# A four-layer graph network: layer 1's first part moved into the edge loop of layer 0

## The chip, the cores and the metric

The kernel runs on one core of a Trainium2 chip. A core has a matrix engine (TensorE, PE in the profile, with its weight loads listed as PEld), a vector engine (VectorE, DVE), an engine for functions (ScalarE, ACT), a general engine (GpSimd, POOL), and SyncE (SP), which here only issues transfers. Each engine works through its own queue in order and waits on semaphores for the others. The metric is device time in microseconds (us), the median of several runs.

## The reference, cut to what matters

There are 4096 nodes with 512 features, and 65536 edges (src, dst). Four layers follow one another, each with a layer norm and a relu ahead of it and its result added to x:

```python
# layer 0
h = relu(layernorm(x)); x = x + gat(h, src, dst)      # 8 heads, then softmax over the 512 features
# layer 1
h = relu(layernorm(x)); x = x + gcn(h)                # relu((D^-1/2 A D^-1/2 h) @ W)
# layer 2
h = relu(layernorm(x)); x = x + message_passing(h)    # two dense layers on every edge
# layer 3
h = relu(layernorm(x)); x = x + gcn_by_destination(h)
```

Layer 0 gives each source node a softmax-weighted sum over its distinct edges: a numerator of 512 columns, a denominator for each of 8 heads. What layer 1 needs for a block of 128 nodes before any edge can be summed, called **layer 1's first part** here, is: numerator by denominator, softmax over the features, add x, layer norm, relu, product with the 512 x 512 weight, and scaling by the root of the node's degree. The result is a row of the table `ytab`, which layer 1's edge loop gathers.

## The kernel before, in words

Nodes are held in 32 blocks (NB) of 128 (P). `acc` is an SBUF array of 32 blocks x 522 columns: 512 sums, 8 denominators, 2 degree columns. Edges are sorted by source in a sorting network that runs beside the first projection. In the 512 columns (tiles) of 128 sorted edges each, 8 tiles make a group of the layer 0 edge loop: 64 groups, in source order, so that group g's sources lie in a window of 128 consecutive nodes, and these windows move forward through the blocks. A window can straddle two blocks, which is why a group is added to `acc` twice (`add_window`, L424), each time with a mask, at a block number read from a register.

`attend` is that loop. Its order is written by hand; within it each engine's queue is the order of the calls. In the step for group g:

- `fetch(g+3)`: 8 indirect gathers on POOL (through the helper `gather`, L412) into `rows`, which has four buffers.
- `turn(g+1)`: PE turns 8 one-hot matrices (L623) into two PSUM banks named `t_ps`; `turned` casts them on ACT (`oh_t`, L631) and selects the source's scores (`of`, L635 on ACT, L636 on DVE).
- `weigh(g, j)`: DVE multiplies two tiles' rows by their weights for 6 heads (L678); `weigh_last` does the other 2 heads on ACT (L672).
- `add_up(j)`: PE adds two tiles to `sum_ps` (L684), for j = 0, 2, 4, 6. These are the four pairs of sums of a group.
- `keep(g-1)`: DVE adds the previous group's sums to `acc` (L424).
- `one_hots(g+2)`: one DVE instruction (L407).
- `source_parts(g+1)`: 8 short matmuls into `e_ps` (L644), after the second pair of sums. `scores(g+1)` reads them on DVE (L650 to L656) and takes the exponent on ACT (L657), and `weights(g+1)` writes the weights (L664, L665), at the end of the step.

So the last product of a group (`weigh(g, 6)`) stands on DVE behind the scores of the next group, and the last pair of sums on PE stands behind that product.

After the loop `layer1_begins` does layer 1's first part in eight rounds of four blocks: it divides (L793), takes the maximum (L795) and the exponent (L798, with the sum of the row as a second output, read by an instruction of its own), adds x (L800), stores x1 (L801), takes mean and variance (L349), norms (L377), turns (L384, L386), multiplies by the weight (`product`, L401), scales (L809) and stores the row of `ytab` (L810). It runs between the two edge loops; no gather runs beside it.

Then `sum_edges` for layer 1 gathers from `ytab` (L412), sums on PE (L768) and adds with `add_window`. Beside it run `Between` (layer 1's end and layer 2's first product, block by block) and `by_destination` (the edge lists in the order of the destination), as generators that are advanced after every second tile.

Of the kernel before, what the change touches and what calls it, by code (L numbers as in the profile page):

```python
# [20 lines left out]
P = 128  # L21
# [13 lines left out]
def kernel(  # L35
# [57 lines left out]
    acc = keep_pool.tile([P, NB, DA], F32, name="acc")  # L93
    dis = keep_pool.tile([P, NB], F32, name="dis")

# [15 lines left out]

    ends = src_pool.tile([P, 2, W], I32, name="ends")
    sg = src_pool.tile([P, 8], F32, name="sg")
    turns = src_pool.tile([P, 7, P], F32, name="turns")
    ones = src_pool.tile([P, P], F32, name="ones")
    shift = src_pool.tile([P, P], F32, name="shift")
    p_f = src_pool.tile([P, 1], F32, name="p_f")

    x1 = dram.tile([N, D], F32, name="x1")
# [136 lines left out]
    def by_destination(pool, ppool):  # L256

        three = pool.tile([P, 3, W], F32, name="three_d")
        for j in range(2):
# [46 lines left out]
    class Side:  # L306


        def __init__(self, *work):
            self.work = list(work)  # L310
# [238 lines left out]
    with tc.tile_pool(name="sort", bufs=1) as sp, tc.tile_pool(name="sort_ps", bufs=1, space=PSUM) as spp, \  # L549
# [28 lines left out]
        nc.vector.tensor_copy(odd[:, 2:3], widest)  # L578
        nc.sync.dma_start(nodes, node.rearrange("p b k h -> p (b k h)"))

    node3 = node_pool.tile([P, NB, 3, 2 * H], BF16, name="node3")
    with tc.tile_pool(name="parts", bufs=1) as lp:
        rest = lp.tile([P, NB, 2 * H], F32, name="rest")
        nc.vector.tensor_copy(rest, node[:, :, 0:2, :].rearrange("p b c h -> p b (c h)"))
        for k in range(3):
            nc.vector.tensor_copy(node3[:, :, k, :], rest)
            if k < 2:
                nc.vector.tensor_sub(rest, rest, node3[:, :, k, :])

    GT = 8  # L590
    ACT_HEADS = 2
# [3 lines left out]
    def attend(ctx):  # L595
        if True:
# [3 lines left out]
            kept = ctx.enter_context(tc.tile_pool(name="edge_keep", bufs=1, space=PSUM))  # L600
            both_ps = kept.tile([P, P + 2 * GT * H], F32, name="both_ps")
            ids_ps = both_ps[:, :P]
            w_ps = both_ps[:, P:].rearrange("p (k t h) -> p k t h", k=2, t=GT)
            nc.scalar.copy(ids_ps, row_i)
# [85 lines left out]


            rows, ohs, sums = {}, {}, {}
            for g in range(-3, groups + 1):
                now = lambda k: 0 <= k < groups
# [35 lines left out]
    one2 = node_pool.tile([P, 2], F32, name="one2")  # L730
# [46 lines left out]

    ytab = dram.tile([N, D], F32, name="ytab")
    def layer1_begins():
# [31 lines left out]

    layer1_begins()
    ptab = dram.tile([N, D], F32, name="ptab")
# [637 lines left out]
```

## Time and profile before

| | us |
|---|---|
| median of 3 runs | 5849.13 (5844.71 to 5850.42) |
| the profiled execution's own time | 5524.6 |
| its span | 5522.8 |
| PE busy in the span | 5110.0 (93%) |
| DVE busy | 3529.2 (64%) |
| ACT busy | 3323.5 (60%) |
| POOL busy | 2910.0 (53%) |
| sums of layer 0's edge loop (L684), first and last start | 256.1 and 897.6 |
| first sum of layer 1's edge loop (L768) | 1067.8 |

Rows of the profile give line, engine, operation, output and inputs, shapes and count; then busy time and the mean duration of one in ns; then the idle time of the engine ahead of these instructions, and what ended it. "issue" is idle time in which the engine waited for nothing that the profile shows. A 32-bit matmul of this kernel appears as two instructions. Matmuls overlap in the queue, so that the mean duration of one is longer than the time that it adds.

### The profile page before, as it was taken

Reading aid. Unit: us, or ns where it says so; the run is one execution under the profiler, and the core shown is the slowest. Engines: PE = TensorE matmul, PEld = TensorE weight load, DVE = VectorE, ACT = ScalarE, POOL = GpSimd, SP = SyncE. Lnnn points to the kernel's source line nnn. Section 1 sums busy time; section 2 is a strip of 40 time slices with the busy share of each in tenths; the row PEclk is TensorE's granted clock in tenths of the full one; section 3 lists DMA queues with packets and bytes.
Section 4 is the critical chain, followed back from the end, with each engine's and each line's share of the span. In section 5 each row is a group of like instructions: output and inputs, shape, how many; then the busy total and the mean of one; then the engine's idle time right before and its main releaser. Section 6 shows DMA issues by size and latency. Waiting matters only on the chain.

```text
span 5522.8 us, 56347 instructions
## 1 busy us (share of the span) xinstructions
PE 5110.0 (93%) x17274; PEld 2739.2 (50%) x17274; DVE 3529.2 (64%) x5696; ACT 3323.5 (60%) x5015; POOL 2910.0 (53%) x2604
## 2 busy tenths in 40 slices
PE   6788887899998999999999999999999899988887
PEld 4477775344443455555555555555555566622222
DVE  8688888333333677777777777777777465633333
ACT  1255555344443788888888888888888434333343
POOL 0177772277774655555555555555554111157776
PEclk9899999999999999999999999999999999999999
DMA  3377775588885655555555555555554211167787
GB/s 103 100 214 214 214 214 180 184 263 269 261 263 180 145 114 114 114 114 114 114 115 114 115 114 115 115 114 114 114 114 84 77 69 65 58 192 210 236 252 222
DMA packets 344871, 841.72 MB, mean 152 GB/s; under 512 B 60272, under 2 KB 76656, under 8 KB 344560
## 3 DMA queue, kind: packets, MB, share of 16 engines
q0 software_dynamic: 237568, 673.35, 49.6%
q1 hardware_dynamic: 106992, 164.66, 8.7%
q8 instruction: 141, 2.31, 0.2%
q14 instruction: 170, 1.39, 0.1%
HBM read 752.62 MB, written 85.20 MB: 152 GB/s over the span
## 4 chain that ended last, share of the span: by engine, by line
PE 69%; DMA 6%; POOL 4%; issue 2%; DVE 1%; ACT 1%; DVEq 0%; SPq 0%; POOLq 0%; ACTq 0%
PE m_ps L401 32%; PE sum_ps L768 9%; DMA g<-ztab,d_src 5%; PE small_ps L967 4%; PE small_ps L994 4%; PE o_ps L401 4%; PE tr_ps L974 4%; PE u_ps L1159 4%; PE pq_ps L868 4%; POOL g L412 4%; PE tr_ps L957 1%; PE tr L1134 1%; PE y_ps L401 1%; DMA g<-ytab,s_dst 0%; ACT h_t L1136 0%
## 5 line engine op out<-in xcount | busy, mean ns | idle before, releaser
L401 PE MATMUL m_ps<-w_sb,h_t 128*128 128x512 f32 x4096 | 1820.8, 592 | 0.5 <-ACT h_t L976 0.5
L401 PEld LDWEIGHTS m_ps<-w_sb,h_t 128*128 128x128 f32 x4096 | 757.5, 190 | 809.1 <-issue 797.8
L768 PE MATMUL sum_ps<-g,oh 128*128 128x512 f32 x2048 | 1026.3, 617 | 135.5 <-DMA g<-ztab,d_src 90.2
L412 POOL DMA_INDIRECT pg<-ptab,d_src x512 | 496.6, 970 | 986.6 <-ACT h_t L976 809.7
L950 POOL DMA_INDIRECT pg<-qtab,d_dst x512 | 880.7, 1720 | 156.4 <-issue 144.1
L768 PEld LDWEIGHTS sum_ps<-g,oh 128*128 128x128 f32 x2048 | 355.7, 191 | 745.0 <-issue 342.4
L412 POOL DMA_INDIRECT rows<-htab,s_dst x512 | 484.5, 946 | 394.3 <-issue 376.7
L412 POOL DMA_INDIRECT g<-ytab,s_dst x512 | 486.0, 949 | 355.6 <-DMA x_mid<-x 180.5
L412 POOL DMA_INDIRECT g<-ztab,d_src x512 | 485.2, 948 | 239.4 <-issue 118.2
L684 PE MATMUL sum_ps<-rows,oh 128*128 128x261 f32 x2048 | 502.8, 393 | 98.7 <-DVE rows L678 98.7
L976 ACT COPY h_t<-tr_ps 128x512 f32<-128x512 f32 x512 | 275.2, 589 | 429.3 <-PE tr_ps L974 429.2
L424 DVE SCALAR_TENSOR_TENSOR acc<-sum_ps,d_half,acc 128x512 f32 x256 | 192.3, 751 | 444.8 <-PE sum_ps L768 425.6
L684 PEld LDWEIGHTS sum_ps<-rows,oh 128*128 128x128 f32 x2048 | 378.0, 192 | 179.0 <-DVE rows L678 124.9
L1026 DVE TENSOR_TENSOR pg<-pg,small_ps 128x512 f32<-128x512 f32 x512 | 318.6, 683 | 186.7 <-PE small_ps L967 150.1
L424 DVE SCALAR_TENSOR_TENSOR acc<-sum_ps,s_half,acc 128x522 f32 (+1 forms) x256 | 193.2, 755 | 375.5 <-PE sum_ps L768 334.4
L994 PE MATMUL small_ps<-parts,oh 128*128 128x512 f32 x1024 | 310.7, 446 | 13.4 <-DVE oh L407 13.4
L988 DVE TENSOR_TENSOR parts<-z,parts 128x1024 fp32r<-128x1024 f32 x256 | 313.6, 1225 | 8.8
L974 PEld LDWEIGHTS tr_ps<-ident,pg 128*128 128x128 f32 x2048 | 240.6, 142 | 145.6 <-issue 145.6
L424 DVE SCALAR_TENSOR_TENSOR acc<-small_ps,d_half,acc 128x512 f32 x256 | 192.3, 751 | 171.6 <-PE small_ps L994 152.3
L1063 DVE TENSOR_TENSOR pg<-pg,qg 128x1024 f32<-128x1024 f32 x256 | 301.4, 1219 | 0.7 <-ACT qg L1060 0.7
L1150 POOL TENSOR_TENSOR h_sb<-h_sb,b_bc 128x1024 f32<-128x1024 f32 x16 | 37.7, 2355 | 453.8 <-PE tr L1134 428.8
L974 PE MATMUL tr_ps<-ident,pg 128*128 128x128 f32 x2048 | 266.3, 273 | 10.8 <-DVE pg L1063 10.8
(278 smaller groups left out, 7982.2 us busy)
## 6 DMA issues: line engine op xcount, KB each, us to landing
xt<-in_x_dram SPq DMA_DIRECT2D x16, 1024.0 KB, 5.8
eg<-in_edge_attr_dram SPq DMA_DIRECT2D x128, 128.0 KB, 2.7
htab<-acc SPq DMA_DIRECT2D x32, 256.0 KB, 2.0
rows<-htab,s_dst POOLq DMA_INDIRECT x512, 3.8
x<-xt SPq DMA_DIRECT2D x8, 1024.0 KB, 4.3
ytab<-acc SPq DMA_DIRECT2D x32, 256.0 KB, 2.1
x_mid<-x SPq DMA_DIRECT2D x32, 256.0 KB, 5.5
g<-ytab,s_dst POOLq DMA_INDIRECT x512, 4.6
```

The lines of the kernel that those rows point to most:

```text
L401: nc.tensor.matmul(ps, h_t[:, k, :], w_sb[:, k0 + k, :], start=start and k == 0, stop=stop and k == KC - 1)
L412: nc.gpsimd.indirect_dma_start(out=dst_ap, out_offset=None, in_=table, in_offset=bass.IndirectOffsetOnAxis(ap=idx, axis=0))
L424: nc.vector.scalar_tensor_tensor(at, ps, half[:, k, i:i + 1], at, op0=OP.mult, op1=OP.add)
L684: nc.tensor.matmul(ps[:, c, :HW], oh[:, j + k, :], rows[:, j + k, c * HW:(c + 1) * HW], start=j + k == 0, stop=j + k == GT - 1)
L768: nc.tensor.matmul(ps, oh[:, j, :], g[:, j, :], start=i % per == 0 and j == 0, stop=i % per == per - 1 and j == U - 1)
L950: nc.gpsimd.indirect_dma_start(out=pg[:, j, :], out_offset=None, in_=qtab, in_offset=bass.IndirectOffsetOnAxis(ap=d_dst[:, t:t + 1], axis= ...
L974: nc.tensor.transpose(h_ps[:, k, :], h[:, j, k * P:(k + 1) * P], ident)
L976: nc.scalar.copy(h_t, h_ps)
L988: nc.vector.tensor_sub(parts[:, 1], m, parts[:, 0].bitcast(F32))
L994: nc.tensor.matmul(ps, oh[:, j, :], parts[j // 2][:, k, j % 2, :], start=j == 0 and k == 0, stop=j == U - 1 and k == 1)
L1026: nc.vector.tensor_add(nxt[:, j], nxt[:, j], ps)
L1063: nc.vector.tensor_mul(h[i][:, half], h[i][:, half], qg[:, half])
```

## The change

Layer 1's first part is no longer called after the edge loop. It is cut into 13 steps per block (class `Block`), and a plan places each step in the loop of `attend`: how many groups after the block's begin, and at which of six places in the step. Block b begins in the step for group 2b + 3, at the latest in that for group 64; six steps without edge work follow the last group so that the last blocks are finished. A block's transposes ("turn") and its product ("multiply") stand at the place "between", which is after the third pair of sums and ahead of the last. PSUM banks for both come from the two `t_ps` buffers. The arithmetic differs in places: the norm's mean comes from a sum that the addition of x gives as a second output, and the variance from a square on ACT with a summed output; norm and relu are one ACT instruction; the roots of variance and degree are taken together, two columns wide, in `scales`, whose second column is now `dis`. x is loaded and x1 stored block by block.

The sort's temporary tiles move to a pool of their own that is closed after the projection, so `by_destination` loads `ends` again.

```diff
-    dis = keep_pool.tile([P, NB], F32, name="dis")
+    scales = keep_pool.tile([P, NB, 2], F32, name="scales")
+    dis = scales[:, :, 1]
...
     def by_destination(pool, ppool):
+        ends = pool.tile([P, 2, W], I32, name="ends_d")
+        for j, of in enumerate((src, dst)):
+            nc.sync.dma_start(ends[:, j, :], of.rearrange("(p c) -> p c", p=P))
+        yield
...
-            both_ps = kept.tile([P, P + 2 * GT * H], F32, name="both_ps")
+            both_ps = kept.tile([P, P + 2 * GT * H + 2 * H], F32, name="both_ps")
...
+            den_ps = both_ps[:, P + 2 * GT * H:].rearrange("p (k h) -> p k h", k=2)
+            wp = ctx.enter_context(tc.tile_pool(name="l1_w", bufs=1))
+            w_sb = load_w(wp, "w_sb", w_l1)
...
+            class Block:
+                xs = {}
+                def __init__(self, b):
+                    self.b, self.row = b, acc[:, b, :D]
+                    for k in range(b, min(b + 2, NB)):
+                        if k not in self.xs:
+                            self.xs[k] = ep.tile([P, D], F32, name="x_row", bufs=3)
+                            nc.sync.dma_start(self.xs[k], x[k * P:(k + 1) * P, :])
+                    self.x = self.xs.pop(b)
+                    self.small = lambda name, n=1: ep.tile([P, n], F32, name=name)
+                def share(self):
+                    self.hn = ep.tile([P, D], F32, name="h_row", bufs=2)
+                    den = den_ps[:, self.b % 2]
+                    nc.vector.reciprocal(den, acc[:, self.b, D:D + H])
+                    nc.vector.tensor_mul(self.hn.rearrange("p (h f) -> p h f", h=H),
+                                         self.row.rearrange("p (h f) -> p h f", h=H),
+                                         den.unsqueeze(2).to_broadcast([P, H, F]))
+                    self.low = self.small("low")
+                    nc.vector.tensor_reduce(self.low, self.hn, axis=AX.X, op=OP.max, negate=True)
+                def exponent(self):
+                    self.whole = self.small("whole")
+                    nc.scalar.activation(self.hn, self.hn, AF.Exp, bias=self.low, accum_out=self.whole)
+                def add(self):
+                    total = self.small("total")
+                    nc.vector.reciprocal(self.whole, self.whole)
+                    nc.vector.scalar_tensor_tensor(self.x, self.hn, self.whole, self.x, op0=OP.mult, op1=OP.add,
+                                                   accum_out=total)
+                    nc.sync.dma_start(x1[self.b * P:(self.b + 1) * P, :], self.x)
+                    self.mean = self.small("minus_mean")
+                    nc.vector.tensor_scalar(self.mean, total, -1.0 / D, None, op0=OP.mult)
+                def spread(self):
+                    self.sq = self.small("squares")
+                    nc.scalar.activation(self.hn, self.x, AF.Square, bias=self.mean, accum_out=self.sq)
+                def variance(self):
+                    self.var = self.small("var", 2)
+                    nc.vector.tensor_scalar(self.var[:, 0:1], self.sq, 1.0 / D, EPS, op0=OP.mult, op1=OP.add)
+                    nc.vector.tensor_copy(self.var[:, 1:2], acc[:, self.b, D + H:D + H + 1])
+                def roots(self):
+                    self.root = self.small("root", 2)
+                    nc.scalar.activation(self.root, self.var, AF.Ln)
+                    nc.scalar.activation(self.root, self.root, AF.Exp, scale=-0.5)
+                def sharpen(self):
+                    r, t, o = self.root, self.small("newton", 2), scales[:, self.b, :]
+                    nc.vector.tensor_mul(t, r, r)
+                    nc.vector.tensor_mul(t, t, self.var)
+                    nc.vector.tensor_scalar(t, t, -0.5, 1.5, op0=OP.mult, op1=OP.add)
+                    nc.vector.tensor_mul(o, r, t)
+                    self.shift = self.small("shift_by")
+                    nc.vector.tensor_mul(self.shift, self.mean, o[:, 0:1])
+                def normal(self):
+                    nc.scalar.activation(self.hn, self.x, AF.Relu, scale=scales[:, self.b, 0:1], bias=self.shift)
+                def turn(self):
+                    self.ps = eps.tile([P, KC, P], F32, name="t_ps")
+                    for k in range(KC):
+                        nc.tensor.transpose(self.ps[:, k, :], self.hn[:, k * P:(k + 1) * P], ident)
+                def turned(self):
+                    self.h_t = ep.tile([P, KC, P], F32, name="h_row_t", bufs=1)
+                    nc.scalar.copy(self.h_t, self.ps)
+                def multiply(self):
+                    self.ps = eps.tile([P, D], F32, name="t_ps")
+                    product(self.ps, self.h_t, w_sb)
+                def put(self):
+                    nc.scalar.activation(self.row, self.ps, AF.Copy, scale=scales[:, self.b, 1:2])
+                def store(self):
+                    nc.sync.dma_start(ytab[self.b * P:(self.b + 1) * P, :], self.row)
+
+            PLAN = {"share": (0, "end"), "exponent": (1, "turned"), "add": (1, "end"), "spread": (2, "first"),
+                    "variance": (2, "summed"), "roots": (2, "turned"), "sharpen": (2, "end"), "normal": (3, "first"),
+                    "turn": (3, "between"), "turned": (3, "weighed"), "multiply": (4, "between"), "put": (4, "end"),
+                    "store": (5, "summed")}
+            begun = {}
+            def blocks(g, place):
+                for b in range(NB):
+                    since = g - min(2 * b + 3, groups)
+                    for step, when in PLAN.items():
+                        if when == (since, place):
+                            if step == "share":
+                                begun[b] = Block(b)
+                            getattr(begun[b], step)()
+                            if step == "store":
+                                del begun[b]
...
-            for g in range(-3, groups + 1):
+            for g in range(-3, groups + 6):
...
                     weigh_last(2, rows[g])
                     weigh(g, 2, rows[g])
+                blocks(g, "first")
                 if now(g - 1):
                     keep(g - 1, sums.pop(g - 1))
                     del rows[g - 1], ohs[g - 1]
+                blocks(g, "summed")
                 if now(g + 1):
                     parts = turned(g + 1, made)
+                blocks(g, "turned")
...
                     add_up(4, rows[g], ohs[g], sums[g])
+                blocks(g, "between")
                 if now(g + 1):
                     u = scores(rows[g + 1], e_ps)
                 if now(g):
                     weigh_last(6, rows[g])
                     weigh(g, 6, rows[g])
+                blocks(g, "weighed")
+                if now(g):
                     add_up(6, rows[g], ohs[g], sums[g])
                 if now(g + 1):
                     weights(g + 1, rows[g + 1], u)
                     weigh_last(0, rows[g + 1])
+                blocks(g, "end")
...
-    layer1_begins()
```

More of the change, by code (lines that the diff above doesn't have):

```diff
@@ L110 @@
     s_half = src_pool.tile([P, 2, NW], F32, name="s_half")
-    ends = src_pool.tile([P, 2, W], I32, name="ends")
-    sg = src_pool.tile([P, 8], F32, name="sg")
-    turns = src_pool.tile([P, 7, P], F32, name="turns")
     ones = src_pool.tile([P, P], F32, name="ones")
-    shift = src_pool.tile([P, P], F32, name="shift")
     p_f = src_pool.tile([P, 1], F32, name="p_f")
+    sorting = ExitStack()
+    sort_pool = sorting.enter_context(tc.tile_pool(name="sorting", bufs=1, side="right"))
+    ends = sort_pool.tile([P, 2, W], I32, name="ends")
+    sg = sort_pool.tile([P, 8], F32, name="sg")
+    turns = sort_pool.tile([P, 7, P], F32, name="turns")
+    shift = sort_pool.tile([P, P], F32, name="shift")
     x1 = dram.tile([N, D], F32, name="x1")
@@ L579 @@
         nc.sync.dma_start(nodes, node.rearrange("p b k h -> p (b k h)"))
+    sorting.close()
     node3 = node_pool.tile([P, NB, 3, 2 * H], BF16, name="node3")
@@ L588 @@
                 nc.vector.tensor_sub(rest, rest, node3[:, :, k, :])
+    ytab = dram.tile([N, D], F32, name="ytab")
     GT = 8
@@ L600, in attend @@
             kept = ctx.enter_context(tc.tile_pool(name="edge_keep", bufs=1, space=PSUM))
-            both_ps = kept.tile([P, P + 2 * GT * H], F32, name="both_ps")
+            both_ps = kept.tile([P, P + 2 * GT * H + 2 * H], F32, name="both_ps")
             ids_ps = both_ps[:, :P]
-            w_ps = both_ps[:, P:].rearrange("p (k t h) -> p k t h", k=2, t=GT)
+            w_ps = both_ps[:, P:P + 2 * GT * H].rearrange("p (k t h) -> p k t h", k=2, t=GT)
+            den_ps = both_ps[:, P + 2 * GT * H:].rearrange("p (k h) -> p k h", k=2)
+            wp = ctx.enter_context(tc.tile_pool(name="l1_w", bufs=1))
+            w_sb = load_w(wp, "w_sb", w_l1)
             nc.scalar.copy(ids_ps, row_i)
@@ L776, in sum_edges @@
             side.finish()
-    ytab = dram.tile([N, D], F32, name="ytab")
     def layer1_begins():
```

## The prediction

> **What bounds the kernel now.** The change touches two stretches, so the stretches were read first: the edge loop of layer 0 (about 256 to 900 us), and the first part of layer 1, which stands alone between it and the next edge loop. Columns: busy us and instructions of PE, weight loads, DVE, ACT, POOL; then granted clock, DMA share, GB/s.
>
> ```profile
> 260.00:898.00 638.00, 547.58 (x3039) 450.42 (x3037) 507.06 (x883) 360.69 (x1388) 469.50 (x497) 0.99 0.74 209
> 899.00:1061.00 162.00, 130.18 (x384) 63.43 (x384) 106.99 (x302) 68.38 (x158) 0.00 (x0) 0.94 0.47 166
> ```
>
> In the second stretch POOL issues nothing: 162 us in which no gather runs. In the first no engine is full by its busy time, so the groups of 400 to 800 us come next, with the waits of PE and of DVE there:
>
> ```profile
> L684 PE MATMUL sum_ps<-rows,oh 128*128 128x261 f32 x1281 | 313.5, 392 | 55.3 <-DVE rows L678 55.3
> L412 POOL DMA_INDIRECT rows<-htab,s_dst x321 | 303.6, 946 | 97.8 <-issue 85.9 <-DVE both_ps L664 5.2 <-DMA rows<-htab,s_dst 4.0
> ...
> L650 DVE TENSOR_REDUCE near<-e_ps 128x128 f32<-128x384 f32 x40 | 22.3, 558 | 16.3 <-PE e_ps L644 15.9
> ```
>
> ```profile
> PE sum_ps L684 <- DVE rows L678: 55.3, 40, 2.5
> ```
>
> ```profile
> DVE u L652 <- DMA rows<-htab,s_dst: 29.7, 34, 1.9
> DVE near L650 <- PE e_ps L644: 15.9, 37, 0.8
> DVE rows L678 <- ACT rows L665: 11.2, 40, 0.3
> ```
>
> Forty groups in 400 us: 10.0 us each. POOL explains that number: 303.6 + 97.8 us for 321 gathers is 1.25 us per gather, and eight make 10.0 us. POOL is the bound, though its busy share says 76%: the 0.30 us between two gathers is its own issue. The chain of waits confirms it: PE waits 1.38 us per group (55.3/40) ahead of the last pair of sums, for the DVE product L678, and DVE had itself waited 0.74 us (29.7/40) for gathered rows and 0.40 us for e_ps. Without waits PE needs (400 - 55.3)/40 = 8.62 us per group. DVE needs 10.0 - 0.74 - 0.40 - 0.05 (a wait for sums) = 8.8 us, of which 8.06 is busy time and the rest is hand-over. So three queues lie close together: POOL 10.0, DVE 8.8, PE 8.6; ACT is busy for 5.7.
>
> For the removed stage, its groups:
>
> ```profile
> L401 PE MATMUL y_ps<-w_sb,h_t 128*128 128x512 f32 x256 | 115.3, 604 | 9.0 <-ACT h_t L386 9.0
> ...
> L800 DVE SCALAR_TENSOR_TENSOR xt<-acc,whole,xt 128x512 f32<-128x512 f32 x32 | 23.3, 740 | 13.4 <-DMA xt<-in_x_dram 7.8 <-issue 5.5
> L798 ACT ACTIVATE acc<-acc,top 128x512 f32<-128x512 f32 x32 | 23.0, 719 | 15.8 <-DVE top L796 8.2 <-DVE xt L800 7.6
> ...
> L795 DVE TENSOR_REDUCE top<-acc 128x1 f32<-128x512 f32 x32 | 21.4, 669 | 0.0
> L793 DVE TENSOR_TENSOR acc<-acc,rden 128x512 f32<-128x512 f32 x32 | 21.0, 679 | 0.0
> ...
> L384 PE MATMUL tr<-ident,hn 128*128 128x128 f32 x128 | 17.5, 282 | 19.3 <-DVE hn L377 19.3
> ```
>
> The mean of a matmul (604 ns) overlaps its neighbour; busy time over count is what it occupies: 115.3/256 = 0.45 us, and the chain has 16 of them in 7.15 us. A product is 8 such instructions: 3.5 us. Four transposes take 4 x 17.5/128 = 0.55 us. The end of the stage, from the timeline:
>
> ```profile
> 1057.14 0.32 SPq L810 DMA_DIRECT2D ytab<-acc  x1
> 1057.52 0.42 SPq L832 DMA_DIRECT2D x_mid<-x  x1
> ...
> 1061.15 0.94 POOL L412 DMA_INDIRECT g<-ytab,s_dst  x1 [180.54 <-DMA x_mid<-x]
> ```
>
> These rows are in order of time: start, duration, engine. From the issue of the last ytab store to the first gather are 4 us; the same will follow the new last store.
>
> **The change, part by part.** *Removed:* everything between the last window added to acc (DVE ends at 899.6) and the last ytab store (1057.14): **157.5 us**.
>
> *Added to the loop:* one block for every two groups, from the end of group 3. Its costs per pair of groups:
> - PE: 0.55 (even group) + 3.5 (odd group) = 4.05 us, all placed ahead of the last pair of sums, where PE now waits 1.38 us.
> - DVE: share is a small reciprocal 0.2 + product 0.68 + maximum 0.67; add is 0.155 + 0.74 + 0.14; variance 2 x 0.145; sharpen 5 x 0.16. Sum 3.7; with hand-overs of 0.03 between dependent ones (the four u instructions start 0.26 apart and last 0.23) 3.95.
> - ACT: exponent and spread 0.72 + 0.19 (accumulator read) each, roots 2 x 0.2, normal 0.65 (between L386's 0.59 and L838's 0.72), turned 0.59, put 0.69: 4.15. ACT is busy 5.7 of 10.0, so 2 x 5.7 + 4.15 = 15.6 per pair; it is hidden, except where it stands ahead of something.
> - SP: an x load, an x1 store and a ytab store of 256 KB each per block. In 400 to 800 us only gathers are issued, so SP is free; the loads run two groups ahead and the stores land in 2 to 4 us (L810, L801). The DMA share rises from 0.74 to about 0.77 (24 MB at the removed stage's rate, 162 x 0.47/26.9 us per MB, is 68 us of 16 engines over 700). Without that cover each late load would stop DVE's add and with it weigh of the next group.
>
> *PE after it:* 2 x 8.62 + 4.05 = 21.3 us per pair. *DVE:* 2 x 8.8 + 3.95 = 21.55. *POOL:* 20.0. **DVE becomes the bound, PE 0.3 us behind, POOL no longer.** The waits for rows vanish; new ones were sought by laying the queues side by side, from the end of weigh(6), with the distances of the timeline at 600 to 620 us (PE: last sums 1.9, transposes 0.9, four tiles' sums 3.5, source parts 0.2, sums 2.0; DVE: 8.8).
> - Odd group: the product ends about 1.3 us after weigh(6), so add_up(6) starts that late and ends at 3.3; DVE meanwhile does sharpen and share (until 2.9), weigh twice (4.7), then keep, which needs those sums: ready. No DVE wait; weigh(6) of the next group ends at 11.2. PE arrives at 10.3 and waits 0.9.
> - Even group: DVE does add (1.5), weigh twice (3.4), keep (5.0), variance (5.3). ACT has turned, weights, two weigh_last and spread ahead of the casts of oh_t and of `of`: about 5.9. Here DVE waits 0.6 for ACT. Weigh(6) ends at 10.8; PE leaves the sums at 8.5 and fills 3.5 with the product.
>
> Pair: 11.2 + 10.9 = **22.1 us** against 20.0. Behind the new wait on ACT stand weigh(4), one_hots, scores and weigh(6), and PE waits for those. The t_ps ring of two banks is now shared with the block: put frees its bank at about 2.6 after weigh(6), PE's next four transposes need it at 3.6. Margin 1 us; were put late, PE's transposes, then the casts, then e_ps would slip.
>
> *A rule weighed.* The row for the addition, L800, is 740 ns, without an accumulator. The Trainium skill ("Vector Engine (DVE) Microarchitecture Reference", section "Points that are easy to get wrong") says that this kind of instruction with two SBUF sources that aren't bf16 runs at half throughput, the read ports leaving none for the accumulator. By rows, an element costs (1219 - 679)/512 = 1.05 ns (L407 against L793), so halving would add 0.54 us. L800 beside L793's 679 shows no halving. The change adds accum_out, which no DVE row here has. Bounds: 0.74 and 1.28 + 0.19 (a read like ACT's). I take 0.74 with 0.1 for the read, within the 22.1; by the rule the pair is 22.7 and the total 17 us worse.
>
> *A second rule.* AF.Square is new. "ScalarE: Activation LUTs", section "Table sets: the hidden batching unit", lists relu, copy, identity and abs as in every set, not Square, and prices a switch at about 2.7 us; the trace's row for a load is 1283 ns, and Ln, Exp and Relu take none in the stage. A switch ahead of spread would make `of` late by 1.3 (row) to 2.7 us (page), and a second is due before roots: pair 23.4 to 24.8, total -41 to +1 or worse. I take no switch, since the other fillers show none.
>
> *Tail:* blocks 30 and 31 finish after the last group. Chain from the last keep: add(30) 1.1, share(31) 1.6, variance and roots(30) 0.8, exponent(31) 0.9, add(31) 1.1, spread(31) 0.9, variance, roots, sharpen 1.8, normal 0.65, then PE, busy with product 30 until about 11.4; turn(31) 0.6, turned 0.6, product 3.5, put 0.7, hand-overs: **17 us**. Before, the last group also waited 3.3 us for the last gathers; with POOL ahead that shrinks by 2.
>
> *Rest:* loading `ends` again is two 256 KB loads on SP in layer 1's loop. DVE's first step of that side work waits some 3 us for them; queued behind it is add_window, which four PSUM banks cover (DVE is busy 78 of 235 us there). Uncovered it costs 3 us once. dis as a strided view, the pool on the right side: nothing, the operands stay 128 x 1.
>
> *Sum:* 30 pairs x 2.1 = +63; last wait -2; stage -157.5 + 17. Total **-80 us**: profiled execution 5524.6 (span 5522.8) to about 5445. The median of the runs shown is 5849.13, 324.5 above the profiled time, and no row says why; I carry the difference as a constant: **5769**. If it is instead a slower PE, by 6%, PE's pair becomes 22.6 plus its wait and the stage 8 us longer: about -55, 5794.
>
> **Rivals.**
> 1. *Overlap closes up* (pair 21.3, PE's own work): DVE's bubbles fill. Total -104 us, 5745. For: POOL's waits go. Against: DVE's 21.55 without waits.
> 2. *The old waits stay* (pair 23.3 to 24.3): PE waits 1.38 again in each group, since weigh(6) is simply last in a queue that got 2 us longer. 2 x 10.0 + 4.05 = 24.05: -22 us, 5828. For: PE waited in all 40 groups. Against: half of that came from rows.
> 3. *Slower.* The pair of groups is a ring, PE to DVE to PE; if the DVE work placed at a group's end, ahead of weigh(0), adds to the ring beside PE's product, the pair is 20.0 + 4.05 + 3.95 = 28: +97 us, 5946. It decides from a pair of 24.75 (140.5 + 2 over 30, above 20.0). For: all those steps do stand ahead of weigh(0). Against: in the odd group PE spends that time in product, sums and transposes, 5 us in all.
>
> **How the numbers follow.** Forecast (pair 21.6 to 22.8): 0.56, own range 5752 to 5792. Rival 1: 0.12. Rival 2: 0.21, of which 0.03 ends within 0.2%. Rival 3 and pairs above 24.75: 0.11, of which 0.02 ends within 0.2% (0.2%, 12 us, is about what a measurement of this kernel can tell from no change). Faster: 0.56 + 0.12 + 0.18 = 0.86; same 0.05; slower 0.09. The range reaches from rival 1 with some margin, 5735, to rival 2's, 5830; left out are about 0.11 above and 0.04 below.
>
> **What would show it.** Gathers of the loop spaced over 1.25 us with waits for buffers (POOL no bound); 11 us from one scores group to the next; PE waits for L678 below 0.6 us per group and DVE waits for rows near zero; DVE about 90% busy in the loop; a wait of DVE on ACT at `of` in every second group; the last sums at about 958 us, the first ytab gather near 981; no table load in the loop. Wrong would be: waits at t_ps or at put, table loads, or an accumulating DVE instruction far above 0.9 us.

## The result, and the profile after

The changed kernel takes **5804.91 us** (median of 7 runs, 5779.73 to 5820.65) against 5849.35 (7 runs, 5844.71 to 5858.02). The ratio is **0.9913**, with a 95% interval of 0.9887 to 0.9939: 44 us less (36 to 66 by that interval), where 80 were forecast. The profiled execution took 5780.2 us, its span is 5778.3.

The numbers can't be understood without one thing: in these times and in this profile the edge loops carry waits that the profile of before does not have. In the runs of the next section the kernel before takes 5846 to 5858 us on one chip, which has such waits, and 5518 to 5523 on three others, which have not (undisturbed chips, below). By its times the result belongs to the first kind, and the profile of before to the second. So the rows below can't be held one by one against those shown before; pairs of runs on one chip can.

First two windows of the changed kernel: from the last sum of layer 0's loop to layer 1's first, and 400 to 800 us. Columns: busy us and instructions of PE, weight loads, DVE, ACT, POOL; then granted clock, DMA share, GB/s.

```profile
1120.00:1152.00 32.00, 16.08 (x40) 7.17 (x38) 6.94 (x27) 14.67 (x36) 5.31 (x6) 0.78 0.41 137
400.00:800.00 400.00, 339.94 (x1617) 260.85 (x1616) 290.53 (x628) 224.98 (x795) 225.71 (x239) 0.92 0.64 189
```

Between the last sum of the one loop and the first of the next lie 32 us instead of 170. But the loop lasts to 1120 us instead of 898, with 30 groups in 400 us (30 rows of L662 below) instead of 40, and no engine is full: PE works 85% of the time, DVE 73%. The groups of 400 to 800 us, with idle time and what ended it:

```profile
L696 PE MATMUL sum_ps<-rows,oh 128*128 128x261 f32 x960 | 255.5, 417 | 57.9 <-DVE u L668 36.3 <-DVE rows L690 13.8 <-issue 7.7
L419 POOL DMA_INDIRECT rows<-htab,s_dst x239 | 226.3, 947 | 174.6 <-PE sum_ps L696 104.0 <-issue 60.6 <-PE t_ps L635 6.6
...
L408 PE MATMUL t_ps<-w_sb,h_row_t 128*128 128x512 f32 x117 | 52.8, 592 | 0.0
...
L662 DVE TENSOR_REDUCE near<-e_ps 128x128 f32<-128x384 f32 x30 | 16.7, 558 | 66.3 <-remote 31.0 <-PE t_ps L770 22.8 <-PE e_ps L656 9.8
```

POOL is no longer the bound: it waits 104 us for PE to free `rows`, as forecast. DVE waits 66 us ahead of `scores` (L662), for signals of PE, and PE 58 us ahead of its sums. Waits of this size at L662 were in no part of the forecast.

### The profile page after: what moved, and what is told of

The parts are those of the page before. It is cut to its first block, busy times and chain, and to the rows that moved or that the text cites. A ratio compares the mean times of both kernels' runs of the same rounds, so it can differ in the third digit from the quotient of the medians.

```text
span 5778.3 us, 56747 instructions
## 1 busy us (share of the span) xinstructions
PE 5151.7 (89%) x17274; PEld 2829.3 (49%) x17274; DVE 3529.1 (61%) x5843; ACT 3371.5 (58%) x5157; POOL 2915.0 (50%) x2604
## 4 chain that ended last, share of the span: by engine, by line
PE 75%; another core or an unknown queue 4%; DVE 4%; issue 4%; ACT 4%; DMA 1%; DVEq 1%; POOL 0%; SPq 0%; ACTq 0%; POOLq 0%
PE m_ps L408 30%; PE sum_ps L887 12%; PE sum_ps L696 5%; PE small_ps L1084 4%; PE small_ps L1111 4%; PE o_ps L408 4%; PE tr_ps L1091 4%; PE u_ps L1276 4%; PE pq_ps L985 3%; ACT oh L863 1%; DVE acc L431 1%; PE t_ps L408 1%; PE tr_ps L1074 1%; PE tr L1251 1%
## 5 line engine op out<-in xcount | busy, mean ns | idle before, releaser
L887 PE MATMUL sum_ps<-g,oh 128*128 128x512 f32 x2048 | 1013.4, 637 | 286.1 <-ACT oh L864 133.3
L887 PEld LDWEIGHTS sum_ps<-g,oh 128*128 128x128 f32 x2048 | 407.8, 204 | 836.5 <-issue 632.5
L696 PE MATMUL sum_ps<-rows,oh 128*128 128x261 f32 x2048 | 539.1, 414 | 153.6 <-DVE rows L690 62.1
L419 POOL DMA_INDIRECT g<-ztab,d_src x512 | 487.0, 951 | 323.7 <-issue 140.5
L696 PEld LDWEIGHTS sum_ps<-rows,oh 128*128 128x128 f32 x2048 | 402.0, 203 | 247.1 <-DVE rows L690 69.4
L863 ACT ACTIVATE oh<-row_i,d_loc 128x128 f32<-128x128 f32 x512 | 162.1, 387 | 231.9 <-remote 131.9
```

Of the source, the lines that this page charges most:

```text
L419: nc.gpsimd.indirect_dma_start(out=dst_ap, out_offset=None, in_=table, in_offset=bass.IndirectOffsetOnAxis(ap=idx, axis=0))
L696: nc.tensor.matmul(ps[:, c, :HW], oh[:, j + k, :], rows[:, j + k, c * HW:(c + 1) * HW], start=j + k == 0, stop=j + k == GT - 1)
L887: nc.tensor.matmul(ps, oh[:, j, :], g[:, j, :], start=i % per == 0 and j == 0, stop=i % per == per - 1 and j == U - 1)
```

## The experiments

The theory going in was the forecast's: DVE's queue sets the pair of groups. Its rival: PE's own work does (rival 1). And, from the profile after: a third term that comes with the chip and not with the change.

**Both kernels on one chip.** No edit.

> The kernel before, unchanged, profiled once more. The profile of before has a span of 5522.8 us, 326 us under its median time, while the profile of the changed kernel (5778.3) agrees with its median. If the first profile was an execution without some delay that the timed ones have, this one should read about 5850, with the edge loop of layer 0 longer than 641 us and layer 3's edge loop, which no line of the change touches, near the 746 us that it takes in the changed kernel instead of 644. If the changed kernel itself brought the delay, this profile repeats 5523 and 641 us.

> The changed kernel, unchanged, profiled once more on the same chip as the last. If the long waits in its loop (865 us from first to last sum, where 700 were forecast) belong to the change, the loop repeats 850 to 880 us. If they come and go with the execution, the loop is between 700 and 800 us and the waits named remote or issue shrink.

Measured on one chip: before 5521.88 us, after 5423.21: 98.7 us less. By the first expectation alone, the kernel before at 5522 again would have meant that the change brings the waits; the second run shows that it does not, with a loop of 670.5 us, shorter than the 700 to 800 expected. A later run of the changed kernel on a third chip gave 5425.33, beside 5517.52 for the kernel before. Stations of both spans, from the first and last start of the sums of each layer:

| us | before | after | difference |
|---|---|---|---|
| start to first sum of layer 0 | 254.2 | 256.1 | +1.9 |
| layer 0's loop, first to last sum | 641.3 | 670.5 | +29.2 |
| to layer 1's first sum | 170.2 | 33.1 | -137.1 |
| layer 1's loop to its end | 686.0 | 690.7 | +4.7 |
| rest | 3768.4 | 3771.0 | +2.6 |
| span | 5520.1 | 5421.4 | -98.7 |

Layer 1's loop is counted here to the first instruction after it. The groups of the changed kernel, 400 to 800 us:

```profile
L419 POOL DMA_INDIRECT rows<-htab,s_dst x314 | 301.9, 961 | 99.8 <-issue 81.9 <-PE sum_ps L696 7.3 <-DMA rows<-htab,s_dst 2.4
L696 PE MATMUL sum_ps<-rows,oh 128*128 128x261 f32 x1219 | 293.5, 388 | 5.2 <-DVE rows L690 5.1
...
L408 PE MATMUL t_ps<-w_sb,h_row_t 128*128 128x512 f32 x156 | 70.2, 592 | 0.0
...
L735 DVE SCALAR_TENSOR_TENSOR x_row<-h_row,whole,x_row 128x512 f32<-128x512 f32 x19 | 14.3, 752 | 0.9 <-DVE whole L734 0.2
...
L648 DVE SCALAR_TENSOR_TENSOR of<-node,s_half,of 128x48 bf16<-128x48 bf16 x38 | 10.2, 269 | 13.3 <-ACT root L752 12.5 <-issue 0.4
```

The window of the same stretch, first of the kernel before and then of the changed one, and two of DVE's waits in the latter:

```profile
400.00:800.00 400.00, 341.23 (x1919) 281.41 (x1919) 322.12 (x560) 228.87 (x880) 302.68 (x320) 1.00 0.76 214
400.00:800.00 400.00, 394.80 (x2059) 308.30 (x2058) 367.66 (x804) 282.95 (x1012) 300.46 (x314) 1.00 0.83 247
```

```profile
DVE of L648 <- ACT root L752: 12.5, 19, 1.0
DVE near L662 <- PE e_ps L656: 2.6, 14, 0.2
```

PE is busy 394.8 of 400 us (10.33 per group) and its wait for the last product is 5.1 us, where it was 55.3 in the profile of before. A group takes 670.5/64 = 10.48 us, a pair 20.95, not 22.1. DVE is busy 92%, and its wait on ACT at `of` is there in every second group, 0.66 us each (forecast 0.6). The pair is close to rival 1's 21.3. That PE is full says it is the bound; the next runs try it.

**Which engine is the bound.** `short_product` leaves out three quarters of the block's product on PE, `less_dve` the maximum and the Newton step on DVE:

```diff
 # short_product, in multiply
-                    product(self.ps, self.h_t, w_sb)
+                    nc.tensor.matmul(self.ps, self.h_t[:, 0, :], w_sb[:, 0, :], start=True, stop=True)
 # less_dve, in share, exponent and sharpen
-                    self.low = self.small("low")
-                    nc.vector.tensor_reduce(self.low, self.hn, axis=AX.X, op=OP.max, negate=True)
...
-                    nc.scalar.activation(self.hn, self.hn, AF.Exp, bias=self.low, accum_out=self.whole)
+                    nc.scalar.activation(self.hn, self.hn, AF.Exp, accum_out=self.whole)
...
-                    nc.vector.tensor_mul(t, r, r)
-                    nc.vector.tensor_mul(t, t, self.var)
-                    nc.vector.tensor_scalar(t, t, -0.5, 1.5, op0=OP.mult, op1=OP.add)
-                    nc.vector.tensor_mul(o, r, t)
+                    nc.vector.tensor_copy(o, r)
```

> The changed kernel with one of the four 128-row parts of each block's product; the other three are left out, so layer 1 gets a quarter of its sum. PE has 2.7 us less per pair of groups, DVE, ACT, POOL and SP have the same. If PE is the bound of the loop: the pair falls from 20.95 to POOL's 20.0 or to DVE's bound, so the loop falls by 20 to 30 us from 671, and PE waits again for L690. If DVE is the bound, as the forecast had it (21.55 us of work without waits): the loop stays within 5 us of 671.

> The changed kernel without the row maximum ahead of the softmax and without the Newton step behind the roots (the softmax is the same by arithmetic, the roots keep ACT's accuracy). DVE has about 1.2 us less per pair of groups, PE the same. If DVE is the bound: the loop falls by about 30 us from 671. If PE is the bound: it stays within 6 us, and the tail behind the loop is 1 to 3 us shorter.

Both ran on one chip, beside the kernel before:

> The kernel before, unchanged, on the chip of the three next runs. If that chip shows the long waits that the first profile of the changed kernel had, this profile tells where the kernel before has them: about 5850 in all, with the three gather loops (layers 0, 1 and 3) some 100 us longer each than in the first profile. If not, it repeats 5520 and a loop of 641 us from first to last sum.

The kernel before took 5522.82 there, and 5521.53 in a run of its own. The changed kernel as it is did not run on this chip; its loop takes 670.1 to 670.5 us on the two others. `less_dve` took 5418.29 us, its loop 669.4: DVE's work fell from 367.66 to 347.82 us in 400, about 1 us per pair, and the loop stayed within about 1 us. (What it gains lies behind the loop, with 28.5 us to layer 1's first sum instead of 33, more than the 1 to 3 expected.) **DVE is not the bound.** `short_product` took 5407.89, its loop 658.4, 12 us less, where 20 to 30 were expected if PE is the bound. Its window:

```profile
400.00:800.00 400.00, 360.92 (x1979) 289.66 (x1978) 370.34 (x810) 282.51 (x1022) 302.86 (x319) 1.00 0.83 251
```

and its waits there:

```profile
POOL rows L419 <- issue: 82.3, 270, 0.3
...
PE sum_ps L696 <- DVE rows L690: 39.0, 59, 1.0
DVE of L648 <- ACT root L752: 12.5, 19, 1.0
POOL rows L419 <- PE sum_ps L696: 3.7, 12, 0.3
```

PE's busy time falls by 2.1 us per pair, 2 x (10.33 - 360.92/38.9), where 2.7 were expected; over 32 pairs that would be 67 us if PE alone counted. The loop gives 12: a pair is 658.4/32 = 20.6, PE waits for the last product again (39.0 us in 59 waits), and DVE, busy 370.34 us with one kind of wait left that counts, the 12.5 us at `of`, is by these rows the engine that now sets the pace. No run takes the work off PE and DVE at once, which would try that last step. POOL is still not it: it waits for next to nothing but its own issue, runs ahead at 1.25 us per gather (319 in 400 us), and its last gather starts at 884.6 us, 30 us ahead of the last sums. **So PE binds the changed loop at 20.95 us per pair, and DVE's queue, with its wait on ACT, lies less than 0.4 us beneath it.** PE and DVE stand in the other order than forecast; DVE's queue is some 1.5 us shorter than the 22.1 given to it.

**The place of transposes and product.** `place_end` puts them at the end of the step, ahead of the next group's first sums:

```diff
-                    "turn": (3, "between"), "turned": (3, "weighed"), "multiply": (4, "between"), "put": (4, "end"),
+                    "turn": (3, "end"), "turned": (4, "first"), "multiply": (4, "end"), "put": (5, "first"),
```

> The changed kernel with the block's transposes and product behind the last pair of sums of the group instead of ahead of it (turned and put follow at the next group's start). If the place matters, because at its old place the product runs while DVE works on the last weigh: PE waits about 1.5 us in one group and 0.8 us in the other for L690 again, the transposes and e_ps of the group after the product come 3.5 us later, a pair takes about 22.6 us where the changed kernel takes 20.95, the loop (first to last sum) is about 720 us where that has 671, and the whole is 45 to 55 us slower than the changed kernel. If only PE's total work counts, the loop is within 5 us of 671.

Measured 5485.23 us on the same chip as the two above: 36 to 38 less than before, 60 to 62 more than the changed kernel on the other two chips of that kind, where 45 to 55 were expected. The loop is 730.2 us, a pair 22.8. The waits, 400 to 800 us:

```profile
POOL rows L419 <- PE sum_ps L696: 61.6, 33, 3.5
ACT acc L781 <- PE t_ps L408: 49.5, 17, 2.9
...
DVE acc L431 <- ACT acc L781: 29.7, 17, 1.8
```

From the groups of the same run comes PE's own wait:

```profile
L696 PE MATMUL sum_ps<-rows,oh 128*128 128x261 f32 x1110 | 268.6, 389 | 22.9 <-DVE rows L690 22.9
```

At the end of the step the product is late for `put`, ACT stands in `put` until it is done, DVE's `keep` waits for ACT, and the last product of weights comes late again: PE waits 22.9 us in 35 groups, 0.66 each, where the changed kernel has 0.13. That is less than the 1.5 and 0.8 expected; the rest of the loss lies in the other waits shown. Between the third and the last pair of sums, the same work fills the time in which DVE finishes `weigh(6)`. The place alone is worth some 60 us, more than half of what the change brings.

**The chip of the times.** No edit; both kernels together on a chip that, by its times, is of the kind on which the result was measured.

> The kernel before once more, for its trace on this chip: about 5520 with a loop of 640 us, or, on a chip with the long waits, about 5850 with a loop near 800.

> The changed kernel, timed in rounds beside the kernel before on one chip. If this chip has the short waits of the last two profiles of the changed kernel's kind, it is 96 to 100 us faster than before (ratio 0.982), as the ledger of the traces gives: loop +29, between the loop and the first gather of layer 1 -138, layer 1 +6. If it has the long waits of the first profile of the changed kernel, the ratio is near 0.991 and the loop is near 865 us.

Before: 5846.26 us with its profile (5851.82, median of 7). After: 5788.94 (5777.08 to 5791.26), ratio 0.9894, 0.9877 to 0.9910. By the same stations, before and after: layer 0's loop 767.1 and 860.6 (+93.5), to layer 1's first sum 169.5 and 31.6 (-138), layer 1 785.3 and 761.3 (-24), rest 3866.6 and 3866.5. In the profiles of the changed kernel taken on this chip layer 1 takes 757 to 762 us, and 784 with the edits below, so that term has a scatter of the size of its difference, and I make nothing of it. The gap between the loops shrinks by as much as elsewhere. The loop's own time is another: it already took 12.0 us per group before the change, where POOL's gathers need 10.0. The waits of the kernel before on this chip, 400 to 800 us:

```profile
DVE acc L424 <- remote: 44.3, 19, 3.1
...
PE sum_ps L684 <- issue: 43.1, 21, 2.9
ACT oh_t L631 <- remote: 41.6, 19, 2.9
POOL rows L412 <- remote: 39.4, 19, 2.2
```

"remote" is a release that the profile can't place. In 19 of the 34 groups, by the second figure of these rows, DVE, ACT and POOL resume together, some 2 us after PE's records show the work that they wait for as done. The timeline has one such place: PE's transposes into `t_ps` are over at 608.06, and ACT's cast of them starts at 610.03.

```profile
607.03 1.03 PE L623 MATMUL t_ps<-ident,oh 128*128 128x128 f32 x8
...
609.98 1.57 DVE L424 SCALAR_TENSOR_TENSOR acc<-sum_ps,s_half,acc 128x522 f32 x2 [2.31 <-remote]
610.03 1.07 ACT L631 CAST oh_t<-t_ps 128x512 bf16<-128x512 f32 x2 [2.16 <-remote]
610.21 0.95 POOL L412 DMA_INDIRECT rows<-htab,s_dst  x1 [2.11 <-remote]
```

The windows of layer 0's whole loop give PE's account, first before and after on the chip of the first pair (`before_again`, `after_again`), then before and after here (`before_c`, `after_timed`):

```profile
254.20:895.50 641.30, 548.29 (x3048) 451.71 (x3048) 509.19 (x885) 363.22 (x1399) 472.59 (x500) 0.99 0.75 209
256.10:926.60 670.50, 651.30 (x3396) 510.42 (x3396) 605.37 (x1308) 463.86 (x1668) 480.27 (x500) 1.00 0.79 234
256.00:1023.10 767.10, 598.96 (x3047) 480.63 (x3048) 513.30 (x885) 361.54 (x1399) 472.14 (x500) 0.92 0.62 175
255.30:1115.90 860.60, 705.58 (x3395) 539.96 (x3396) 609.30 (x1308) 468.64 (x1668) 474.02 (x500) 0.93 0.62 183
```

There, PE is idle for 93 us before the change and 19 after it; here, for 168 and 155. So here the added PE work, some 107 us, fills almost none of PE's idle time: by this reading that time is spent waiting for something that comes late whatever PE has to do meanwhile, and so the work is added to it. Layer 3's loop, whose code the change does not touch, takes about 100 us more on this chip than on the others too.

A rival is PE's clock: 0.92 and 0.93 are granted over this loop here, 0.99 and 1.00 there. It is part of the excess. After the longer pauses of PE, as the one from 615 to 617.5 us, the sums run at half the clock for some 3 us:

```profile
615.00:617.50 2.50, 0.00 (x0) 0.00 (x0) 2.15 (x6) 0.69 (x4) 1.88 (x2) 1.00 0.79 205
618.00:621.00 3.00, 3.00 (x8) 2.28 (x8) 1.82 (x2) 2.24 (x10) 1.59 (x2) 0.50 0.80 221
```

With that, PE is busy 599 us instead of 548 before the change and 706 instead of 651 after it. That is 51 and 54 us of the excess, nearly the same in both kernels, so it isn't what makes the change dearer here; and from 608 to 610 us, where the signals are late, the clock stood at 1.00. That PE's signals come late is read from the records. Why they do on one chip and not on three others, and whether it belongs to that chip or to something that ran beside it, no run here shows, and it stays open.

**The end of the loop and the start of layer 1.** Two details missed the forecast: the last blocks took longer, and layer 1 some 5 us more. `warm_late` and `warm_again` are one kernel: two matmuls without use behind the transposes of block 30 and behind the product of block 29, after the last group, and the lines that load and use `ends` moved 40 steps back in layer 1's side work; `ends_late` has the second edit alone.

```diff
     def by_destination(pool, ppool):
+        for _ in range(40):
+            yield
         ends = pool.tile([P, 2, W], I32, name="ends_d")
...
                 def turn(self):
...
+                    if self.b == NB - 2:
+                        self.warm()
+                def warm(self):
+                    ps = eps.tile([P, D], F32, name="t_ps")
+                    for k in range(2):
+                        nc.tensor.matmul(ps, ident, w_sb[:, k, :], start=k == 0, stop=k == 1)
                 def multiply(self):
...
+                    if self.b == NB - 3:
+                        self.warm()
```

> The changed kernel with two edits. PE gets two extra products of the identity with parts of the weight (4 instructions, 1.8 us, into a bank that nobody reads) in each of its two pauses behind the last group, so that it isn't idle ahead of block 30's product. And by_destination waits for 40 steps before it loads ends again. If the 6.6 us of block 30's product (3.6 elsewhere) come from PE's clock after its pauses, it takes 3.6 here and the last ytab store comes some 3 us earlier after the last sums. If the reload, which lands 16 us after its issue beside the 2 MB weight and holds back DVE, ACT's one-hots and the first gathers, costs the 6 us that layer 1 is longer than before, layer 1 takes 692 us instead of 698 from first gather to its end. Together 7 to 9 us faster than the changed kernel. If neither is on the path: within 2 us of it.

On the chip of the times: 5800.41 us (5783.01 to 5808.19) beside 5788.94 of the changed kernel, where 7 to 9 us less were expected; ratios 0.9902 (0.9883 to 0.9921) and 0.9894. The intervals overlap: this tells nothing.

> The changed kernel once more, to be read beside the other two runs of this call. On a chip on which the kernel before takes 5520 us: 5423, layer 0's loop ends (last sum of L696 starts) at 926.6, first sum of layer 1's loop at 959.7, end of layer 1 at 1650.4. On a chip on which the kernel before takes about 5850: 5777 to 5805, loop end 1116 to 1120, layer 1's first sum 1147 to 1152.

> Two matmuls of an identity with the weight behind the transposes of block 30 and behind the product of block 29, only in the steps after the last group, so that PE does not stand idle there; and the second load of the edge list is used 40 steps later in layer 1's loop. Theory (PE's clock falls in its pauses at the end, and DVE's wait for the edge list costs the start of layer 1's loop): on a chip on which the kernel before takes 5520 us, the product of block 30 takes 3.6 instead of 6.6 us, layer 1's first sum comes 2 to 3 us earlier than in the changed kernel, and layer 1's loop is 3 to 5 us shorter: 5415 to 5418. Rival (both lie beside waits that are there anyway): product shorter, but the last store of ytab within 1 us and the whole within 2 us of the changed kernel. On the other kind of chip the scatter of some 10 us hides it.

> The second load of the edge list alone is used 40 steps later. Theory (DVE's wait of 31 us for it holds up layer 1's sums): layer 1, from its first sum to its end, takes 3 to 5 us less than the 690.7 of the changed kernel, the part before it is unchanged. Rival (four PSUM banks cover the wait, and the 5 us come from gathers and transfers that are slower): within 1 us of the changed kernel.

On one undisturbed chip, before 5517.52: changed kernel 5425.33, `ends_late` 5420.63, `warm_again` 5418.24. (Where the kernel before ran twice on such a chip, its times lie within 1.3 us of each other.) PE at the end of the loop, changed kernel:

```profile
927.64 3.70 PE L408 MATMUL t_ps<-w_sb,h_row_t 128*128 128x512 f32 x8 [0.67 <-ACT h_row_t L774]
933.54 0.66 PE L770 MATMUL t_ps<-ident,h_row 128*128 128x128 f32 x4 [2.20 <-ACT h_row L765]
935.70 6.70 PE L408 MATMUL t_ps<-w_sb,h_row_t 128*128 128x512 f32 x8 [1.50 <-ACT h_row_t L774]
```

and with the matmuls between:

```profile
928.50 3.70 PE L410 MATMUL t_ps<-w_sb,h_row_t 128*128 128x512 f32 x8 [0.68 <-ACT h_row_t L783]
932.04 1.88 PE L779 MATMUL t_ps<-w_sb,ident 128*128 128x512 f32 x4
...
936.61 3.65 PE L410 MATMUL t_ps<-w_sb,h_row_t 128*128 128x512 f32 x8
```

After pauses of 2.20 and 1.50 us the product of block 30 takes 6.70 us; without them 3.65. The granted clock from 936 to 942 us, first of the changed kernel and then with the matmuls between, is 0.52 and 1.00:

```profile
936.00:942.00 6.00, 6.00 (x8) 2.36 (x8) 0.15 (x1) 0.81 (x1) 0.00 (x0) 0.52 0.00 0
936.00:942.00 6.00, 5.27 (x16) 2.28 (x15) 0.81 (x5) 2.49 (x5) 0.00 (x0) 1.00 0.00 1
```

The time from the last sum of layer 0 to the first of layer 1 is then 3.0 us shorter (29.9 against 32.9). From the last addition to `acc` to the last store it is 16.8 us, where the changed kernel had 19.8. The Trainium skill ("TensorE: Matmul & The Clock Gate", section "Part 1: The HAM clock gate (the "warmup" mystery)") says that the clock is halved after a window of some 3.4 us in which PE was idle, until it has been busy as long. The rows agree in kind, with 1.8 times the duration; but neither pause alone was 3.4 us long, 0.66 us of transposes lay between them, and that was not enough to hold the clock.

The second edit: layer 1 takes 684.9 us in `ends_late` and 685.5 in `warm_again`, against 691.2 unchanged and 686.0 before the change. DVE had waited for `ends` there, as the changed kernel's waits of 957 to 1000 us (`after_again`) show:

```profile
DVE three_d L267 <- DMA ends_d<-in_dst_dram: 31.3, 2, 30.7
```

The load itself did not move: it is issued at 950.8 us in `after_again` and at 954.1 in `ends_late`, ahead of layer 1's first sum in both, and lands 16.3 to 16.8 and 16.7 us later. What moved is its use: DVE's first cast of it starts at 1063.8 us instead of 967.3, so that DVE's queue no longer stands behind a load on its way.

`warm_again` is 7.1 us under the changed kernel in single runs beside each other and beats both kernels there, at 0.982 of the kernel before; on the chip of the times its gain can't be told.

## Why the prediction came out as it did

The time, 5804.91, lies in the range, 36 us above the forecast, and faster is right. Its terms did less well than their sum, so the nearness is in part luck.

- **The removed stage and the tail, -140.5.** Right: 157.5 - 19.7 = 137.8 on undisturbed chips, and the gap shrinks by 137 to 138 on both kinds. The tail of 17 us was 19.7 to 19.8 because the clock's loss in PE's pauses was not in it; without these pauses it is 16.8.
- **The loop, +63 with a pair of 22.1 and DVE as the bound.** Wrong on undisturbed chips: +29, a pair of 20.95, PE the bound. The sizes of both queues failed. For DVE, the 21.55 was some 1.6 too long. Where DVE sets the pace (`short_product`) its pair is 20.6: 370.34/38.9 x 2 = 19.0 of busy time, 0.65 of wait on ACT and 0.9 of hand-overs. So the added work takes 2.9 of busy time beyond 2 x 8.06, not 3.95: the steps' own means in `after_again` (0.08 to 0.75 us) still add up to 3.9, but in the records they overlap with their neighbours. And "the rest is hand-over", 0.74 per group, was in part idle time of a loop in which POOL set the pace (in the kernel before, on the chip of `place_end`, 11.9 us in 400 ahead of the products and 8.1 at `of`), and closed up to 0.45. The wait on ACT was found in the right place and at the right size. For PE, the addition of 4.05 is 3.6: per group PE is busy 341.23/40 = 8.53 us before and 394.80/38.2 = 10.33 after. The 8.62 was a little high as well: in the profile of before it took in some slowed sums (granted clock 0.99 in that window). PE's full pair is 2 x 10.33 + 0.27 of waits = 20.93, which is the loop. Rival 1 had mechanism and pair nearly right and got 0.12.
- **"I carry the difference as a constant."** This is the step behind the result. The 324.5 us between the profile and the median are the excess that the other chip shows, of which 126 lay in the very loop that the change fills (767 against 641). There PE's idle time stays, rival 2's mechanism: for its case it had a pair of twice the old group plus the 4.05 added, which by 12.0 per group is 28.0; the loop shows 26.9. The loop costs 93.5 us there instead of 29, and -138 + 93.5 leaves -44 where layer 1 does not help (it helps by 24 in `after_timed`, by 1 in `warm_late`). The alternative that the forecast named, a slower PE, is there in part: the sums' median is 383 ns on both chips, but a part of them runs at half the clock, and PE's busy time in this loop is 9% longer. That is 51 of the 126 us; the rest is waiting, and it is the waiting that the added work does not fill.
- **That forecast and result lie near each other** is therefore in part luck, two errors of opposite sign: the loop was given 34 us more than it takes where nothing is late (63 against 29), and nothing for the 64 us more that it takes where PE's signals are (93.5 against 29).
- **Reload of `ends`, "uncovered it costs 3 us once".** Uncovered it was, and it cost 6 (691.2 against 684.9): the load landed 16 us after its issue, beside layer 1's other loads, not 3, and DVE's queue stood before it.
- **The two rules.** No switch of tables appears in the loop for Square (ACT's spread takes 707 ns, the exponent 706, in `after_again`). For the accumulating addition, rows of 752 ns (L735) and 83 ns for the read of the accumulator stand against 740 without it: what the Trainium skill ("Vector Engine (DVE) Microarchitecture Reference", section "Points that are easy to get wrong") says of half throughput does not show here; the forecast's 0.74 plus 0.1 did hold.
- **The signs named.** Held where nothing is late (`after_again`): gathers waiting for buffers (a little), PE's waits for the last product gone (0.13 us per group), DVE about 90% busy, the wait at `of`, no load of tables. Missed: 11 us per group (10.48), and with it 958 and 981 us for last sums and first gather (926.6 and 952.2).

## What to carry to other kernels

When an engine that is not the bound is given work, its spare time can be spent only as far as its waits are for something that keeps coming at its own pace; count what it needs in a stretch without waits, and expect the sum of busy times of the fullest engine, if the new work lies where that engine waits now (moving it by one place cost 60 us here). When the profiled execution and the timed runs differ by several per cent, the difference is not a constant to be added: ask which loop it sits in, and whether the idle time that the change wants to fill is made of the same waits. At the end of such a loop the matrix engine's pauses cost twice, once as idle time and once in the slower work behind them.

## What the runs showed of the hardware

Three things not expected. Runs on different chips differ in more than a clock: on three chips the kernel before took 5518 to 5523 us, on one 5846 to 5858, with PE's signals in layer 0's loop some 2 us late to three engines at once (44.3 us of DVE's, 41.6 of ACT's and 39.4 of POOL's waits in 400 us), while the dense products keep their mean of 592 ns. Pauses of PE that are shorter than 3 us can be followed by stretches at half the granted clock: 2.5 us idle and then 0.50 from 618 to 621 us on that chip, and 2.20 and 1.50 us idle ahead of a product of 6.70 us instead of 3.65 on another. And a 256 KB load that took its place beside a stage's other loads landed 16.3 to 16.8 us after its issue, where the loads of x in the loop before it, of the same size, landed in 4.3.
